# Order of three side works in a long-convolution and low-rank FFN kernel: low-rank steps, modulation rows, kernel reversal

## The chip, the cores and the metric

The kernel runs on one core of a Trainium2 chip. The metric is the device time of one execution in microseconds (us), the median of several runs. Engines are called as in the profile: PE is the matrix engine (TensorE), PEld its weight loads, ACT ScalarE, DVE VectorE, POOL GpSimd, SP the engine that issues most of the DMAs.

## The reference

x has 4 batches of 1024 rows of 2048 columns (4096 rows). Cut to what matters:

```
mod = (silu(c) @ wmod).reshape(4, 6, 1, 2048)      # six sections: sa, ca, ga, sb, cb, gb
ga, gb = sign(.) * max(abs(.), 0.25)
h = layernorm(x) * (1 + ca) + sa
x = x + ga * (causal_conv(h, K) + D * h)           # K: S4 kernel of length 2048, made on the chip
h = layernorm(x) * (1 + cb) + sb
x = x + gb * (h @ W.T + bias + sum_e coeffs_e * scales_e * (h @ A_e.T) @ Bf_e.T)
```

The convolution runs along the 2048 columns of each row. wmod is 2048 by 12288 in 32-bit floats (96 MiB).

## The kernel before

**Blocks.** The 4096 rows are 32 blocks r of 128 rows. A block goes through four works: `stats` (mean and variance, DVE), `conv_prep` (normalize to n, 16 PE transposes tp, ACT scales them to t, ACT and DVE split t and sums of pairs into 16-bit high and low parts hc and hs), `conv_mm` (the convolution as products with Toeplitz tiles) and `conv_post` (store y, square sum on ACT, L660, for the second layernorm). The square of `conv_post` overwrites the block's x, so the next load into that x slot waits for it.

**Convolution.** `conv_mm` works on two halves q. Each half has three families of products: family 0 into ya (L614), copied by ACT to qs (L627); family 2 into yb, summed with qs by DVE (L631); family 1 on top of ya, which must wait for the qs copy. Each product is made of three 16-bit passes. A block has 41,472 columns of 128x128 products. `tick()` is called nine times in a block, and once after it; `PLAN` says what each tick lets in: N (transposes of the next block), S (`step()`), P (`conv_post` of the block before), T and F (statistics and start of block r+2).

**Start.** Blocks 0 to 2 (`EARLY`) are convolved while the modulation rows still stream in. A section of wmod is 16 rows (`mod_load`, 1 MiB each by SP; `mod_mm`, four 32-bit products on PE, L317). Section 1 (ca) comes first. Sections 0 (sa) and 2 (ga) are paced by `pace`: one row per `ROWC` columns of convolution. The row buffers are three in pool wm and two in pool wms; section 2 uses only wm. The convolution kernel is made by `toeplitz`: a load kb from memory (POOL queue), its reversal on PE (kbps, L263) into kb, then the high and low tiles kh and kl (L284, L285). When section 2 is complete, `mod_gate` makes the gate, `gate_tile` spreads it over partitions (gps, L674; gat, L675), `conv_late` (L650, L651) applies it to blocks 0 to 2, and `conv_post` frees their x slots for blocks 4 and on.

**Low-rank work.** `rest()` is a generator of 191 steps: `prep_lora` (la is loaded and squared, L432; lb is loaded by ACT's queue, L441, scaled, L445, and split into lbh and lbl), eight `merge` of 15 steps (products lps with W, split and stored to wcd), and after each second step one row of the modulation sections 4, 3 and 5. `step()` advances it from within the ticks. When it ends, `early()` opens the pools of the FFN. It must have ended by block 30 (`LEFT0`).

**FFN.** From about 960 us on: 16 units of 256 rows by two column halves, seven products each (fX, fY, fZ, L750).

**Order.** A scheduler orders each engine's instructions from the program order, priorities and dependencies. `tc.issue_after(ins)` keeps an instruction behind `ins` if both are on the same engine; it adds no semaphore. Engines take their instructions in order, so one that waits holds what stands behind it.

Of the kernel before, what the change touches and what calls it, by code (L numbers as in the profile page):

```python
# [19 lines left out]
MUL, ADD, SUB = ALU.mult, ALU.add, ALU.subtract  # L20
# [4 lines left out]
P = 128  # L25
# [9 lines left out]
class Net:  # L35
# [288 lines left out]
    def mod_column(self, pool, home, name, plus_one):  # L324

        nc, v = self.nc, self.nc.vector
        row = pool.tile([P, 512], F32, tag="mg0", name="mrow")
        nc.scalar.copy(row, self.modps)
        ps = self.tps.tile([P, 4, P], F32, tag="t", name="mtp")
        for c in range(4):  # L330
            nc.tensor.transpose(ps[:, c, :], row[:, ds(P * c, P)], self.ident)
        col = home.tile([P, NC, NB], F32, tag=name, name=name)
        src = ps.rearrange("p c (q r) -> p q c r", r=32)[:, :, :, 0:NB]
        dst = col.rearrange("p (q c) b -> p q c b", c=4)
        v.tensor_scalar(dst, src, plus_one, None, ADD)
        return col
# [259 lines left out]
    def conv_mm(self, pl, hs, x, tick, early, pace=lambda n: nullcontext()):  # L596
        nc, v = self.nc, self.nc.vector
        hc, hs = hs
        y = pl["y"].tile([P, D], F32, tag="y", name="y")
        yv = y.rearrange("p (j e t) -> p j e t", e=2, t=P)  # L600
        if not early:
            gv = self.gat.rearrange("p (j e t) -> p j e t", e=2, t=P)
        sums = pl["sm"].tile([P, 2], F32, tag="sums", name="sums")

        def family(ps, f, q, first):
            pf = ps.rearrange("p j t -> p (j t)")
            last = 4 * q + 3
            for i in range(last + 1):
                o = P * max(0, i - 4 * q)
                k0 = P * max(0, 4 * q - i)  # L610
                with pace(3 * (512 - o)):
                    for x, z in ((0, 0), (0, 1), (1, 0)):
                        h = hs[x][:, i] if f == 0 else hc[x][:, 2 * i + 2 - f]
                        nc.tensor.matmul(  # L614
                            pf[:, o:512], h, self.kf[f][z][:, ds(k0, 512 - o)],
                            start=first, stop=(i == last and (x, z) == (1, 0)), skip_group_check=True,
                        )
                        first = False
                if i == 3 and q == 1:
                    tick()  # L620

        for q in range(2):
            jj = slice(4 * q, 4 * q + 4)
            pa = self.acc.tile([P, 4, P], F32, tag="a", name="ya")
            family(pa, 0, q, True)
            qs = pl["t"].tile([P, 4, P], F32, tag="qs", name="qs")
            nc.scalar.copy(qs, pa)  # L627
            tick()
            pb = self.acc.tile([P, 4, P], F32, tag="a", name="yb")
            family(pb, 2, q, True)  # L630
            v.tensor_tensor(yv[:, jj, 1, :], pb, qs, ADD)  # L631
            if not early:
                v.tensor_tensor(yv[:, jj, 1, :], yv[:, jj, 1, :], gv[:, jj, 1, :], MUL)
            tick()
            family(pa, 1, q, False)
            sl = ds(1024 * q, 1024)
            if early:
                nc.scalar.copy(yv[:, jj, 0, :], pa)
            else:
                v.tensor_tensor(yv[:, jj, 0, :], pa, gv[:, jj, 0, :], MUL)  # L640
                v.scalar_tensor_tensor(y[:, sl], y[:, sl], 1.0, x[:, sl], MUL, ADD, accum_out=sums[:, q : q + 1])  # L641
            tick()
        return y, sums
# [167 lines left out]
ACC, TPS = 5, 2  # L811
PLAN = ("PNSL", "NL", "NSL", "NTL", "SL", "SL", "SL", "SL", "FSL", "SSL")
LPLAN = ("LL", "LL", "LL", "LL", "L", "0", "")
R0 = 5
WM, WMS = 3, 2
ROWC = 3000
EARLY = 3
X0 = 11
LEFT0 = 30
# [12 lines left out]
def net(ctx: ExitStack, tc: tile.TileContext, io):  # L832
    nc = tc.nc
    k = Net(ctx, tc, io)
# [10 lines left out]
    pl = {}  # L845
# [6 lines left out]
    def section(sec, pools):  # L852
        for q in range(16):
            if q == 0:
                k.mod_begin()
            k.mod_mm(k.mod_load(pools[q % len(pools)], sec, q), q)
            yield
        if sec == 0:
            k.sa = k.mod_column(msm, k.kpool, "sa", 0.0)
            k.hinv = k.fold_scale(msm, k.ca, k.sa, "fs1")  # L860
        elif sec == 1:
            k.ca = k.mod_column(msm, k.kpool, "ca", 1.0)
        elif sec == 2:
            k.gas, (k.gad,) = k.mod_gate(msm, "gad")
        elif sec == 4:
            k.cb = k.mod_column(msm, k.cst, "cb", 1.0)
        elif sec == 3:
            k.sb = k.mod_column(msm, k.cst, "sb", 0.0)
        else:
            _, k.gbd = k.mod_gate(msm, "gbd", io["bias"])  # L870
        yield
# [8 lines left out]
    def take(g, n):  # L880
        for _ in range(n):
            next(g, None)
# [10 lines left out]
    xs, hs, sts, ys = {}, {}, {}, {}  # L893

    def prep(r, shift=True):
        return k.conv_prep(pl, r, xs[r], sts.pop(r), hs, shift)

    def load(r):
        if r < 4:
            with tc.issue_after(k.lastw.ins):  # L900
                xs[r] = k.conv_load(pl, r)
        else:
            xs[r] = k.conv_load(pl, r)

    def stats(r):
        sts[r] = k.stats(pl, xs[r], "1")
# [9 lines left out]
    k.early_scale(msm)  # L916
    load(1)
    rows = (x for sec, w in ((0, (wms, wmp)), (2, (wmp,))) for x in section(sec, w))
    for r in range(2):
        stats(r)  # L920
        take(prep(r, False), 9)
    take(rows, 1)
    with tc.issue_after(k.last.ins), tc.high_priority():
        take(toe, 2)
    take(rows, 1)
    cols = [0]

    def pace(n):

        cols[0] += n  # L930
        while cols[0] >= ROWC:
            cols[0] -= ROWC
            take(rows, 1)
        return tc.issue_after(k.last.ins)

    for r in range(2):
        load(r + 2)
        ys[r] = k.conv_mm(pl, hs.pop(r), xs[r], lambda: None, True, pace)
    stats(2)
    take(prep(2), 9)  # L940
    k.shift_conv(msm)
# [5 lines left out]
    def rest():  # L947
        mods = (x for sec in (4, 3, 5) for x in section(sec, (wmp,)))
        n = 0
        for _ in mer:  # L950
            yield
            n += 1
            if n % MR == 0:
                next(mods, None)
                yield
        for _ in mods:
            yield
        k.ginv = k.fold_scale(msm, k.cb, k.sb, "fs2", k.winv)
        yield

    fill = rest()
    p2l = ExitStack()
    pr, wc, lf = {}, {}, {}
# [15 lines left out]
    def early():  # L979
        right.close()  # L980
        for name, bufs in (("w", 1), ("l", 8), ("t", 1), ("s", 1), ("x2", 1)):
            pr[name] = pool(p2, "p2" + name, bufs, "right")
        load_w(0, ORDER[0])
# [7 lines left out]
    calls = [0]  # L991

    def step():
        calls[0] += 1
        if r < R0 and calls[0] % 2:
            return
        if "w" not in pr and next(fill, 0) == 0:
            early()

    stats(3)  # L1000
# [18 lines left out]
    for r in range(EARLY, 32):  # L1019
# [6 lines left out]
        if r == LEFT0:  # L1026
            while "w" not in pr:
                step()
            lgen = next_left(0)
# [3 lines left out]
        def tick():  # L1033
            for a in next(plan):
                if a == "S":
                    step()
                elif a == "P" and post:
                    k.conv_post(pl, *post)
                elif a == "L" and r >= LEFT0:
                    take(lgen, 1)  # L1040
                elif a == "N":
                    take(nxt, 1)
                elif a == "T" and r + 2 < 32:
                    stats(r + 2)
                elif a == "F" and r + 2 < 32:
                    follow.append(prep(r + 2))
                    take(follow[0], 1)
# [102 lines left out]
```

## Time and profile before

| | |
|---|---|
| median of 3 runs | 2140.63 us (2140.62 to 2143.34) |
| profiled execution | 2145.74 us, its span 2143.8 us |
| PE busy | 2080.1 us, 97% of the span |
| DVE, ACT busy | 1308.9 us (61%), 927.3 us (43%) |
| mean granted PE clock | 0.986 of full speed |
| DMA | 484 MB, 226 GB/s over the span |

The span is from the first to the last instruction. A busy share is an average over stages: the rows, the convolution blocks and the FFN have different limits. In the lists, a number in square brackets is the idle time of the engine ahead of an instruction, with what ended it; a wait line gives who waited for whom, the total, how often, and the longest.

### The profile page before, as it was taken

The numbers are of one execution on the slowest core, as the hardware profiler recorded it, in microseconds if no ns is written. First come the engines' busy times: TensorE is split into PE (matmuls) and PEld (weight loads), VectorE is DVE, ScalarE is ACT, GpSimd is POOL, SyncE is SP. The second block draws the span as 40 slices with busy tenths as digits, with TensorE's granted clock in tenths as the row PEclk, the third lists the DMA queues.
The fourth block names the chain that finished last, engine by engine and source line by source line (L and its number), as shares of the span: only waits on it lengthen the run. The fifth ranks groups of instructions, "written<-read, shape, count | busy, mean of one in ns | idle before, by whom it ended". The sixth has DMA issues, their size and how long they took to land.

```text
span 2143.8 us, 28420 instructions
## 1 busy us (share of the span) xinstructions
PE 2080.1 (97%) x11113; PEld 1026.8 (48%) x11113; DVE 1308.9 (61%) x2351; ACT 927.3 (43%) x1697; POOL 6.2 (0%) x18
## 2 busy tenths in 40 slices
PE   6897999999999999999999999999999999999998
PEld 2343555545455555654545545545444444444444
DVE  5646988998979999666565565565433333332323
ACT  1344776677657877655454454455200000000000
POOL 0000000000000000000000000000000000000000
PEclk8999999999999999999999999999999999999999
DMA  9887667786776454397565564564794545454542
GB/s 383 357 331 266 245 215 277 285 309 255 269 281 238 187 177 168 110 380 265 179 245 189 188 241 181 202 239 177 275 345 164 189 155 166 163 173 162 176 157 69
DMA packets 127236, 484.11 MB, mean 226 GB/s; under 512 B 13608, under 2 KB 13768, under 8 KB 95998
## 3 DMA queue, kind: packets, MB, share of 16 engines
q1 hardware_dynamic: 126192, 477.55, 61.4%
q10 hardware_dynamic: 526, 2.63, 0.3%
q8 instruction: 87, 1.43, 0.3%
q0 software_dynamic: 384, 2.11, 0.2%
q14 instruction: 47, 0.39, 0.1%
HBM read 326.94 MB, written 155.30 MB: 225 GB/s over the span
## 4 chain that ended last, share of the span: by engine, by line
PE 70%; DVE 13%; DMA 8%; ACT 6%; issue 2%; SPq 0%; ACTq 0%; DVEq 0%
PE fZ L750 23%; PE fY L750 15%; PE fX L750 15%; PE ya L614 6%; PE yb L614 3%; PE tp L700 2%; PE modps L317 2%; DMA wm<-in_wmod 2%; PE lps L486 2%; ACT x L660 2%; DVE hc L593 1%; DVE wch L514 1%; ACT t L582 1%; DVE st L540 1%; DVE y L641 1%
## 5 line engine op out<-in xcount | busy, mean ns | idle before, releaser
L750 PEld LDWEIGHTS <-lf 128*128 128x128 f16 x5376 | 526.0, 98 | 620.5 <-issue 0.9
L750 PE MATMUL fZ<-w,lf 128*128 128x512 f16 x2304 | 514.1, 379 | 0.6 <-ACT p L758 0.6
L750 PE MATMUL fX<-w,lf 128*128 128x512 f16 x1536 | 342.1, 379 | 0.0
L750 PE MATMUL fY<-w,lf 128*128 128x512 f16 x1536 | 342.1, 379 | 0.0
L614 PEld LDWEIGHTS <-hc 128*128 128x128 f16 x2304 | 215.9, 98 | 213.6 <-issue 49.1
L768 DVE TENSOR_TENSOR xo<-xo,gb 128x512 f32<-128x512 f32 x128 | 87.5, 689 | 237.6 <-DMA xo<-x1d 225.6
L614 PE MATMUL ya<-kh,hc 128*128 128x512 f16 (+3 forms) x768 | 192.5, 328 | 10.1 <-ACT qs L627 9.9
L582 ACT ACTIVATE t<-tp,sa,ca 128x128 f32<-128x128 f32 x480 | 188.6, 471 | 19.6 <-PE tp L578 19.2
L614 PE MATMUL ya<-kh,hs 128*128 128x512 f16 (+3 forms) x768 | 195.6, 329 | 1.1 <-DVE kh L284 0.6
L614 PE MATMUL yb<-kh,hc 128*128 128x512 f16 (+3 forms) x768 | 194.0, 329 | 1.3 <-DVE y L640 1.2
L758 ACT COPY p<-fZ 128x512 f32<-128x512 f32 x64 | 37.3, 583 | 293.7 <-PE fZ L750 275.3
L614 PEld LDWEIGHTS <-hs 128*128 128x128 f16 x1152 | 107.0, 98 | 111.0 <-issue 35.2
L702 ACT ACTIVATE gt<-tp,sb,cb 128x256 f32<-128x256 f32 x256 | 125.0, 576 | 62.9 <-PE tp L700 61.3
L758 ACT COPY p<-fX 128x512 f32<-128x512 f32 x32 | 18.8, 586 | 305.5 <-PE fX L750 211.2
L317 PE MATMUL modps<-wm,sct 128*32 128x512 f32 x768 | 116.6, 657 | 22.8 <-DMA wm<-in_wmod 22.8
L614 PE MATMUL ya<-kl,hs 128*128 128x512 f16 (+3 forms) x384 | 126.4, 329 | 1.9 <-DVE kl L285 1.9
L614 PE MATMUL yb<-kl,hc 128*128 128x512 f16 (+3 forms) x384 | 126.3, 329 | 0.0
L614 PE MATMUL ya<-kl,hc 128*128 128x512 f16 (+3 forms) x384 | 125.8, 327 | 0.0
L773 DVE TENSOR_TENSOR fin<-fX,gb 128x512 f32<-128x512 f32 x32 | 22.1, 692 | 126.9 <-PE fX L750 126.8
L593 DVE TENSOR_TENSOR hc<-t,hc 128x512 f16<-128x512 f32 x128 | 87.4, 683 | 10.5 <-ACT hc L592 9.9
L578 PE MATMUL tp<-ident,n 128*128 128x128 f32 x512 | 80.6, 284 | 12.1 <-ACT t L582 6.6
L486 PE MATMUL lps<-lbh,lac 128*128 128x512 f16 x256 | 86.3, 379 | 3.1 <-ACT lbh L460 2.4
(265 smaller groups left out, 2220.0 us busy)
## 6 DMA issues: line engine op xcount, KB each, us to landing
wm<-in_wmod SPq DMA_DIRECT2D x96, 1024.0 KB
lfd<-lf SPq DMA_DIRECT2D x112, 512.0 KB
lf<-lfd SPq DMA_DIRECT2D x112, 512.0 KB
x<-in_x SPq DMA_DIRECT2D x32, 1024.0 KB
x1d<-y SPq DMA_DIRECT2D x32, 1024.0 KB
x<-x1d SPq DMA_DIRECT2D x32, 1024.0 KB
xo<-x1d SPq DMA_DIRECT2D x128, 256.0 KB
out<-xo SPq DMA_DIRECT2D x128, 256.0 KB
```

Of the source, the lines that this page charges most:

```text
L317: self.last = self.nc.tensor.matmul(self.modps[32 * g : 32 * g + 32, :], self.sct[:, j].rearrange("p r b -> p (r b)"), w[:, ds(512 * g, 512)],
L486: nc.tensor.matmul(ps, la[:, x, k, h], y[:, k, osl], start=(n == 0), stop=(n == 5))
L578: nc.tensor.transpose(tp[:, k], n[:, ds(P * (c0 + k), P)], self.ident)
L582: nc.scalar.activation(t[:, k], tp[:, k], AF.Identity, bias=self.sa[:, c, b : b + 1], scale=self.ca[:, c, b : b + 1],)
L593: v.tensor_tensor(lo[:, sl], src, hi[:, sl], SUB)
L614: nc.tensor.matmul(pf[:, o:512], h, self.kf[f][z][:, ds(k0, 512 - o)], start=first, stop=(i == last and (x, z) == (1, 0)), skip_group_chec ...
L660: nc.scalar.activation(x, y, AF.Square, bias=mn, accum_out=sq)
L700: nc.tensor.transpose(tp[:, c, r], xs[r][:, ds(P * (c0 + c), P)], self.ident)
L702: nc.scalar.activation(t[:, c0 + c], tp[:, c], AF.Identity, bias=self.sb[:, c0 + c, b : b + 1], scale=self.cb[:, c0 + c, b : b + 1],)
L750: nc.tensor.matmul(ps[name], lf[i][:, k, x, :], wc[i][k // 4][:, k % 4, y, :], start=(first and n == 0), stop=(n == 3 * HC - 1), skip_grou ...
L758: nc.scalar.copy(t, ps[name])
L768: v.tensor_tensor(x, x, self.gbias[:, h], ADD)
```

## The change

1. Low-rank steps. Before, `step()` advanced the low-rank work at every second call while r was under R0 = 5, and at every call from then on. Now, while r is under R0 = 6, it does so at every third call and only for r over `EARLY` = 3, so in blocks 4 and 5; those steps are traced behind the last qs copy (`k.lasta`, ACT) and the last sum (`k.lastv`, DVE) of the running block.
2. Rows. One modulation row per 2400 convolution columns instead of 3000.
3. Reversal. The two toeplitz steps (kbps, and kh and kl) are traced after the transposes of block 0, behind the last transpose of `mod_column`, without high priority; statistics and transposes of block 1 come after them. Before, they came after both blocks and behind the first row of section 0, with high priority.
4. The load of x for blocks 2 and 3 is traced after the convolution of blocks 0 and 1 instead of before it.

```diff
-            nc.tensor.transpose(ps[:, c, :], row[:, ds(P * c, P)], self.ident)
+            self.last = nc.tensor.transpose(ps[:, c, :], row[:, ds(P * c, P)], self.ident)
...
-            nc.scalar.copy(qs, pa)
+            self.lasta = nc.scalar.copy(qs, pa)
...
-            v.tensor_tensor(yv[:, jj, 1, :], pb, qs, ADD)
+            self.lastv = v.tensor_tensor(yv[:, jj, 1, :], pb, qs, ADD)
...
-R0 = 5
+R0 = 6
-ROWC = 3000
+ROWC = 2400
...
-    for r in range(2):
-        stats(r)
-        take(prep(r, False), 9)
-    take(rows, 1)
-    with tc.issue_after(k.last.ins), tc.high_priority():
+    stats(0)
+    take(prep(0, False), 9)
+    with tc.issue_after(k.last.ins):
         take(toe, 2)
-    take(rows, 1)
+    stats(1)
+    take(prep(1, False), 9)
+    take(rows, 2)
...
     for r in range(2):
+        ys[r] = k.conv_mm(pl, hs.pop(r), xs[r], lambda: None, True, pace)
         load(r + 2)
-        ys[r] = k.conv_mm(pl, hs.pop(r), xs[r], lambda: None, True, pace)
...
     def step():
-        calls[0] += 1
-        if r < R0 and calls[0] % 2:
-            return
-        if "w" not in pr and next(fill, 0) == 0:
+        if r < R0:
+            calls[0] += 1
+            if r > EARLY and calls[0] % 3 == 0:
+                with tc.issue_after(k.lasta.ins), tc.issue_after(k.lastv.ins):
+                    next(fill)
+        elif "w" not in pr and next(fill, 0) == 0:
             early()
```

## The prediction

> **What bounds the kernel now.** I read the page first (busy shares), then the stage table (windows), then in the stage with the densest waits the waits of TensorE (PE) and the timelines of ACT, SP and PE. PE is busy 97% of the span:
>
> ```profile
> PE 2080.1 (97%) x11113; PEld 1026.8 (48%) x11113; DVE 1308.9 (61%) x2351; ACT 927.3 (43%) x1697; POOL 6.2 (0%) x18
> ```
>
> The change adds and removes no matrix product, so only PE's idle time (63.7 us) and its slow-clock time can move. The stage table (us, then busy time of PE, PEld, DVE, ACT, POOL, granted clock, DMA share, GB/s) says where they lie:
>
> ```profile
> 0.00:54.00 54.00, 34.14 (x173) 12.28 (x174) 30.69 (x114) 5.91 (x9) 3.58 (x12) 0.80 0.96 382
> 54.00:176.00 122.00, 112.02 (x690) 48.24 (x689) 58.81 (x124) 45.82 (x117) 1.86 (x4) 0.93 0.87 335
> 176.00:214.20 38.20, 26.94 (x145) 12.49 (x142) 28.28 (x64) 18.36 (x26) 0.00 (x0) 0.90 0.74 265
> 214.20:650.00 435.80, 427.03 (x2608) 221.90 (x2608) 385.36 (x809) 308.19 (x631) 0.35 (x1) 0.98 0.72 264
> 650.00:850.00 200.00, 192.74 (x1194) 108.76 (x1187) 189.41 (x408) 147.04 (x305) 0.41 (x1) 1.00 0.54 200
> 850.00:960.00 110.00, 109.56 (x647) 61.57 (x646) 72.22 (x130) 69.71 (x136) 0.00 (x0) 1.00 0.60 230
> ```
>
> Until 54 nothing is edited. In 54 to 176 the 32 weight rows of sections 0 and 2 stream in beside blocks 0 to 2: PE idles 10.0 us. In 176 to 214 (block 3) it idles 11.3 of 38.2 us, the worst stretch. From 214 to 960 it idles 16.5 us in 746; the FFN after 960 is untouched. Block 3, PE's waits (total, times, longest), then ACT, SP and PE in time:
>
> ```profile
> PE ya L614 <- ACT qs L627: 6.8, 1, 6.8
> PE tp L578 <- DVE n L557: 3.3, 1, 3.3
> ...
> 177.60 0.43 ACTq L441 DMA_DIRECT2D lb<-in_BfT  x1
> 178.08 0.59 ACT L638 COPY y<-ya 128x512 f32<-128x512 f32 x1 [0.28 <-PE gps L674]
> 189.34 2.00 ACT L445 ACTIVATE lb<-lb,lwt 128x2048 f32<-128x2048 f32 x1 [10.68 <-DMA lb<-in_BfT]
> 191.25 0.57 ACT L627 COPY qs<-ya 128x512 f32<-128x512 f32 x1
> ...
> 195.69 1.99 ACT L660 ACTIVATE x<-y,mn 128x2048 f32<-128x2048 f32 x1
> ...
> 197.80 0.35 SPq L562 DMA_DIRECT2D x<-in_x  x1
> ...
> 191.86 0.59 PE L614 MATMUL ya<-kh,hc 128*128 128x512 f16 x1 [6.75 <-ACT qs L627]
> ```
>
> The low-rank preparation (prep_lora) put L445, which needs the 2 MiB load of lb, ahead of block 3's qs copy. ACT stood 10.7 us; qs, ready to be copied when PE stopped at 185.1, ran at 191.25, and PE stood 6.75 us. It also held back L660 (its input mn was there at 188.8; it ran at 195.69), after which alone the next input tile x can load (197.80). That load feeds block 4's statistics, n, and the transposes at 214.2, where PE waits again.
>
> **What the Trainium skill says.** "TensorE: Matmul & The Clock Gate", Part 1 (the HAM clock gate): after an idle window of about 3.4 us PE runs at half rate until it has been busy as long. The trace agrees: after the 6.75 us gap a 128x512 matmul takes 0.63 us instead of 0.38, until 196.6; gaps of 0.6 to 1.5 us at 105 to 123 (PE 75% busy) left the clock at 1.00. "DMA: Bandwidth & Descriptors", Where 436 GB/s comes from: 435 GB/s is the ceiling of a core's ports. The trace's full slices show 415 to 431, so a 1 MiB row costs at least 2.47 us.
>
> **The change, part by part.**
>
> (1) *Low-rank steps.* A block calls step() 9 times. Before, blocks 3, 4, 5 advanced the low-rank work by 4, 5, 9 steps; now by 0, 3, 3: 12 of its 191 steps come later, and it ends in block 26 instead of 25. In the order of the changed program la's squares (L432) stand at block 4's end, lb's load right behind them, and L445 only behind block 5's second qs, some 20 us later, so the 10.7 us transfer is covered by block 5. The DVE instructions L437 (stood 5.2 us for lws at 163 to 168) and L52 to L438 also leave block 3; all its other ACT and DVE instructions keep their order.
>
> Time of block 3 from its gate product (gps, G=176.05) to the transposes of block 4 (214.2), before: 38.15 us. After, on DVE from the timeline's durations: two gat 2.7 (first gps done at G+1.2), L650 4.0, two gat 5.5, L651 6.7, two L650 9.1, two L651 11.5, mn 11.6 (before 12.7). ACT is free: L660 and its accumulator read, 2.18, end at 13.8 (before 21.8): 8.0 us earlier. The load then takes as long as before, at most 7.0 us (197.80 to the statistics at 204.82): 20.6. From the first bn_stats to the end of n DVE takes 9.3 us (204.82 to 214.14): 29.9. **Gain 38.15 - 29.9 = 8.2 us.** PE's own work there is gps and first part 12.9, rest of the convolution 8.4, three rows 3.2: 24.5. So what is late next is n, and PE will wait about 5.4 us at block 4's transposes. Bounds: 13.6 us if only PE's work counted, 4 us if the load lands 4 us later in a busier DMA queue.
>
> Added waits: the steps' ACT and DVE instructions in blocks 4 and 5 queue behind lasta and lastv. Behind them wait only later low-rank work, and on ACT block 5's qs behind L432 (3.8 us); PE has yb's 1.6 us before it needs that: 0 to 2.2 us, taken 0, as ACT is 68% busy there. The first lps product waited 2.45 us for lbh; now its last half of lbl stands behind block 6's last sums, about 4.5 us against 3.2 us of rows and transposes on PE: 1.3 to 3, taken 2: **-0.5 us.** Every DMA of the steps (la and lb 2 MiB each, we, wm rows) moves along with them; SP's queue in blocks 4 and 5 holds only x loads and y stores and four rows. In block 26 the 12 steps fall into 850 to 960, where DVE is 66% and PE idles 0.4 us of 110: nothing. The number of full blocks (some 20) and so their about 1 us of idle each (7.3 in 200 us) stays. That cover gone, it costs 1 to 2 us.
>
> (2) *A row per 2400 columns.* A block has 41,472 convolution columns; 32 rows took 96,000, now 76,800. PE per row: 2400 columns at 0.427 ns (32,256 took 13.77 us after the last row), 1.02, and the row itself 1.06: 2.1 us, under the 2.47 us that DMA needs. So DMA bounds this stage and PE waits about 0.5 us per row. Before, from row 0 (58.16) to row 31 (161.2) DMA moved 34 MiB in 103 us, 11.8 of them idle; 2.68 each otherwise. Now 33 MiB (the x of block 3 falls behind the rows), with about half of the idle time (the hole at 69 to 75 shrinks as row 2 no longer stands behind the first convolution pieces; the one at 135 to 141 shrinks as gsp is split): 33 x 2.68 + 6 = 94.4, so the last row ends at 153.7. Behind it are 51,456 columns (22.0 us) and 16 transposes (2.1): gps at 177.8, **+1.7 us.** Bounds: -3 (no DMA holes) to +6 (holes as before).
>
> (3) *Reversal behind the first transposes.* kbps now runs when kb lands (47.34 + 10.1 = 57.4) rather than behind row 0. But ACT's second kb copy is queued behind the last group of block 0's transposes, so kh comes at about 69.0 (before 68.1) and kl ends at 71.5 (before 71.06). PE does row 2 meanwhile. 0, between -2 and +2.
>
> (4) *Later x loads.* x of block 2 goes behind 16 more rows on SP; its n is ready about 0.8 us after PE asks: hidden by the DMA wait of the next row. x of block 3 is issued behind the last row; it needs 2.7 us to land, then 5.5 for statistics and n and about 5 of the gate's and L414's DVE work, against 10.9 us of columns ahead of its transposes: 0 to +2.5, taken 0. On POOL kb and gsb keep their places.
>
> Sum: -8.2 - 0.5 + 1.7 = -7.0. The profiled execution took 2145.74 (span 2143.8 and 1.9 around it) and becomes 2138.7; the median shown is 5.1 lower, so 2140.63 - 7.0 = **2133.6 us.**
>
> **The rivals.**
> - *The rows cost what block 3 wins* (chance 0.20). For it: DMA share 0.87 already in 54 to 176. Against: the holes come from PE's late release of row buffers, which denser rows relieve. With +6 instead of +1.7 and n late by 2: 2140.
> - *The clock falls in the row stage, slower* (0.13). PE will be about 75% busy between 90 and 150. At 42 to 54 it was 60 to 63% busy and the clock 0.65 to 0.72; at 75% it held. A cold episode costs about 2.5 us (192 to 198 at 0.62) of 6; three eat the gain, and six give 2133.6 + 15 = 2149. It decides from three on.
> - *The stall stays in another place* (0.05): lb's load runs into block 5 or 6 and L445 again holds a qs. For it only that the transfer took 10.7 us; against, some 20 us of ACT work in between. 2141, no change.
>
> **How the numbers follow.** 0.2% (4.3 us) is about what a measurement of this kernel tells from no change. The likeliest case (0.62) has its own range 2126 to 2136. The row rival is half a step inside no change (0.15 of its 0.20, the rest faster); the lb rival 0.03 no change, 0.02 slower; the clock rival slower. Faster 0.67, same 0.18, slower 0.15. The range 2124 to 2145 leaves out the clock rival and a tail below.
>
> **What would show it.** ACT's wait for lb of 10.7 us and PE's 6.8 us for qs vanish; x for block 4 is issued about 14 us after gps, not 21.8; PE then waits some 5 us for n; gps starts at 175 to 181; PE's waits for wm after 54 grow from 5.8 us to 9 or more. Wrong if PE's clock between 90 and 150 falls under 0.9, if gps starts after 182, or if 214 to 960 (746 us, 16.5 of idle) changes by over 4 us.

## The result and the profile after

The changed kernel takes 2140.32 us (median of 20 runs), the kernel before 2142.42 us in its 20 runs beside them. The ratio is 0.9994 with a 95% interval of 0.9985 to 1.0003: no change that the measurement can tell (one disturbed run of 2204 us is left out of the ratio; the others lie between 2134.8 and 2146.6). Forecast was 7.0 us less. The profiled execution took 2140.44 us, its span 2138.5 us. It lies at its kernel's median; the profiled execution of the kernel before (2145.74) lies 3.3 us above the median of 20 runs, so not all of the 5.3 us between the two spans is the change's.

The busy shares, then the rows of the stage table (length, busy time of PE, PEld, DVE, ACT, POOL, granted clock, DMA share, GB/s):

```profile
PE 2078.8 (97%) x11113; PEld 1024.8 (48%) x11113; DVE 1309.8 (61%) x2351; ACT 925.3 (43%) x1697; POOL 6.2 (0%) x18
```

```profile
54.00:176.00 122.00, 105.77 (x651) 43.21 (x650) 55.99 (x117) 39.47 (x107) 1.86 (x4) 0.94 0.90 349
176.00:214.20 38.20, 32.09 (x187) 16.75 (x184) 32.63 (x71) 12.74 (x25) 0.00 (x0) 0.96 0.57 209
214.20:650.00 435.80, 428.60 (x2617) 223.76 (x2617) 385.38 (x814) 315.37 (x644) 0.34 (x1) 0.99 0.70 262
650.00:850.00 200.00, 194.50 (x1203) 108.51 (x1202) 193.10 (x410) 154.92 (x319) 0.41 (x1) 1.00 0.57 213
850.00:960.00 110.00, 109.56 (x641) 60.98 (x639) 73.06 (x129) 66.90 (x125) 0.00 (x0) 1.00 0.62 239
```

The windows stand still while the work moved, so what the rows tell is the idle time: in 54 to 176 PE idles 16.2 us where it idled 10.0, and in 176 to 214.2 only 6.1 where it was 11.3. What block 3 won, the row stage lost. From 214.2 to 960 PE idles 13.1 us in place of 16.5. From the first mtp (PE's transposes behind section 1) to gps PE runs 693 matmuls in both profiles and is busy 113.1 us before and 112.7 after; the 6 us between them are idle time (10.0 and 16.2 us).

The last row, gps and block 4's transposes on PE before:

```profile
161.22 1.06 PE L317 MATMUL modps<-wm,sct 128*32 128x512 f32 x8 [0.26 <-DMA wm<-in_wmod]
...
176.05 1.94 PE L674 MATMUL gps<-mg,ident 128*128 128x512 f32 x4
...
214.20 1.97 PE L578 MATMUL tp<-ident,n 128*128 128x128 f32 x8 [3.28 <-DVE n L557]
```

After, PE's waits from 54 to block 4's first transposes, then PE, ACT, SP and DVE in time (start, duration, instruction, in brackets the idle time ahead of it and what ended it):

```profile
PE modps L317 <- DMA wm<-in_wmod: 7.8, 6, 3.0
PE tp L578 <- DVE n L557: 6.1, 1, 6.1
PE kbps L263 <- DMA kb<-kd: 4.1, 1, 4.1
PE ya L614 <- DVE kh L284: 2.6, 1, 2.6
```

```profile
58.87 6.34 PE L263 MATMUL kbps<-kb,rev 128*128 128x512 f32 x8 [4.06 <-DMA kb<-kd]
...
157.19 1.06 PE L317 MATMUL modps<-wm,sct 128*32 128x512 f32 x8 [0.91 <-DMA wm<-in_wmod]
...
182.16 1.94 PE L674 MATMUL gps<-mg,ident 128*128 128x512 f32 x4
...
193.70 2.00 ACT L660 ACTIVATE x<-y,mn 128x2048 f32<-128x2048 f32 x1 [5.53 <-DVE mn L658]
...
195.82 0.35 SPq L562 DMA_DIRECT2D x<-in_x  x1
...
210.90 1.33 DVE L557 TENSOR_SCALAR n<-x,mv,rs 128x2048 f32<-128x2048 f32 x1
...
212.28 1.97 PE L578 MATMUL tp<-ident,n 128*128 128x128 f32 x8 [6.11 <-DVE n L557]
```

The two stalls of block 3 are gone: no wait of ACT for lb, no 6.8 us of PE for qs. L660 now waits only for mn, x is loaded 13.7 us after gps, and block 4's transposes start 30.1 us after gps (38.15 before, 29.9 forecast). But gps starts at 182.16, not at 176.05 (before) or 177.8 (forecast). So block 4 starts only 1.9 us earlier. The forecast had it at 177.8 + 29.9 = 207.7, which is 6.5 us earlier. The last row ends at 158.25 where 153.7 was forecast; the stretch behind it is the forecast's (23.9 us against 24.1). The question is the row stage.

### The profile page after: what moved, and what is told of

Same layout as the page of the kernel before. It is cut to its first block, busy times and chain, and to the rows that moved or that the text cites. A ratio compares the mean times of both kernels' runs of the same rounds, so it can differ in the third digit from the quotient of the medians.

```text
span 2138.5 us, 28420 instructions
## 1 busy us (share of the span) xinstructions
PE 2078.8 (97%) x11113; PEld 1024.8 (48%) x11113; DVE 1309.8 (61%) x2351; ACT 925.3 (43%) x1697; POOL 6.2 (0%) x18
## 4 chain that ended last, share of the span: by engine, by line
PE 57%; issue 25%; DVE 3%; DMA 2%; ACT 1%; POOLq 0%; SPq 0%; POOL 0%; DVEq 0%
PE fZ L750 23%; PE fY L750 15%; PE fX L750 15%; PE tp L700 2%; PE ya L614 1%; DMA gb<-gbd 1%; PE yb L614 1%; DMA w<-wcd 0%; DVE y L641 0%; ACT x L660 0%; DMA x<-x1d 0%; DVE wch L514 0%; DVE lf L713 0%; DVE st L540 0%; DVE y L640 0%
## 5 line engine op out<-in xcount | busy, mean ns | idle before, releaser
L317 PE MATMUL modps<-wm,sct 128*32 128x512 f32 x768 | 118.4, 666 | 24.2 <-DMA wm<-in_wmod 24.1
```

Source lines behind the costliest of these rows:

```text
L317: self.last = self.nc.tensor.matmul(self.modps[32 * g : 32 * g + 32, :], self.sct[:, j].rearrange("p r b -> p (r b)"), w[:, ds(512 * g, 512)],
```

## The experiments

Theory A: the low-rank steps win what was forecast, and one of the other edits gives it back in blocks 0 to 2. Its rivals change in the course of the runs. Each kernel was timed beside the kernel before. Single executions reach the first mtp at 50.8 to 54.6 us, and one profile is one draw; so the table counts from that mtp, and the ratios, not the profiles, decide. The last three columns are us: from the first mtp to the end of the last row, from there to gps, and from gps to block 4's first transposes.

| kernel | steps | columns per row | reversal | x loads | ratio to before (95%) | mtp to last row's end | to gps | to block 4's tp |
|---|---|---|---|---|---|---|---|---|
| before | old | 3000 | old | old | 1 | 109.3 | 13.8 | 38.1 |
| changed | new | 2400 | new | late | 0.9994 (0.9985 to 1.0003) | 105.0 | 23.9 | 30.1 |
| e8, the same | new | 2400 | new | late | 0.9994 (0.9986 to 1.0003) | 103.6 | 25.5 | 30.2 |
| e1 | new | 3000 | old | old | 0.9967 (0.9956 to 0.9979) | 107.8 | 13.6 | 31.0 |
| e2 | old | 2400 | new | late | 0.9992 (0.9980 to 1.0004) | 105.3 | 29.3 | 30.6 |
| e3 | new | 3000 | new | late | 0.9982 (0.9974 to 0.9991) | 112.0 | 14.8 | 31.1 |
| e4 | new | 2400 | old | late | 0.9986 (0.9977 to 0.9996) | 99.7 | 24.8 | 30.0 |
| e5 | new | 2400 | old | old | 0.9993 (0.9984 to 1.0001) | 107.3 | 21.7 | 30.8 |
| e6 | new | 3000 | new | old | 0.9969 (0.9957 to 0.9981) | 109.6 | 13.6 | 29.9 |
| e7 | new | 3000 | old | late | 0.9965 (0.9953 to 0.9977) | 109.9 | 14.8 | 30.6 |
| e9 | new | 3400 | old | old | 0.9939 (0.9927 to 0.9952) | 110.1 | 8.4 | 29.3 |
| e10, five buffers | new | 2400 | new | late | 0.9975 (0.9967 to 0.9982) | 101.1 | 24.9 | 30.4 |
| e11, half rows | new | 2400 | new | late | 0.9943 (0.9925 to 0.9960) | 91.0 | 25.8 | 31.9 |
| e12 | new | 3700 | old | old | 0.9960 (0.9947 to 0.9973) | 114.3 | 4.2 | 30.7 |
| e13 | new | 3400 | new | late | 0.9988 (0.9978 to 0.9997) | 124.2 | 8.4 | 29.0 |
| e14 | old | 3400 | old | old | 0.9994 (0.9986 to 1.0002) | 108.4 | 8.4 | 36.7 |
| e15 | new | 3400 | new | old | 0.9958 (0.9944 to 0.9971) | 109.4 | 8.4 | 30.2 |
| e16 | new | 3400 | old | late | 0.9992 (0.9985 to 0.9998) | 118.0 | 8.4 | 29.8 |

0.001 of the ratio is 2.1 us. Every kernel with the new steps has 29 to 32 us from gps to block 4.

### e1 to e4: the steps alone, and the change with one part taken back

e1 is the kernel before with the steps only; e2 is the changed kernel with the old `step()` and R0; e3 and e4:

```diff
-ROWC = 2400
+ROWC = 3000
```

```diff
-    stats(0)
-    take(prep(0, False), 9)
-    with tc.issue_after(k.last.ins):
-        take(toe, 2)
-    stats(1)
-    take(prep(1, False), 9)
-    take(rows, 2)
+    for r in range(2):
+        stats(r)
+        take(prep(r, False), 9)
+    take(rows, 1)
+    with tc.issue_after(k.last.ins), tc.high_priority():
+        take(toe, 2)
+    take(rows, 1)
```

> The kernel before with the low-rank steps alone changed (no step in block 3, three each in blocks 4 and 5); rows at 3000 columns, reversal and x loads as before. Theory A (the steps win what was forecast, the new row stage of blocks 0 to 2 gives it back): block 3's gate product starts where it did (176 +-1.5 us), from it to block 4's first transposes about 30 us in place of 38.2, and the time is 7 to 8.5 us below before (ratio 0.9960 to 0.9967): faster than the whole change. Rival B (the steps win nothing in the end, since the low-rank work or another wait comes late elsewhere): ratio 0.999 to 1.000, with the same 30 us in block 3 and 5 to 8 us more in 214 to 960.

> The whole change without its low-rank part: rows at 2400 columns, new place of the reversal, later x loads, but the old steps. Theory A: gate product at 181 to 183 us, the 38 us to block 4's transposes back, and the time 5 to 6 us above before (ratio 1.0023 to 1.0028). Rival B: gate product late as well, but the time within 2 us of before, since the stage's delay is absorbed later. Rival C (the gate product's 182 in the one profile was scatter, the row stage costs nothing): 177 to 179 and ratio 1.000 to 1.001.

> The whole change with 3000 columns per row again. If the denser rows are what makes blocks 0 to 2 late (the forecast's rival), the gate product comes back to about 176 to 177 us and the ratio to before is 0.9965 to 0.9975. If the reversal's new place (kb waited for at about 59 us, first rows of section 0 seven us later) is what costs, 3000 columns make it later still, 182 to 185 us, and the ratio is 0.999 to 1.001.

> The whole change with the old order around the reversal: both blocks' transposes first, a row ahead of the reversal. If the reversal's new place costs the 4 to 5 us by which the last row came later than worked out, row 0 runs at 58 to 63 us again, the last row ends at about 154, the gate product starts at 177 to 178.5 us and the ratio to before is 0.9962 to 0.9972. If the denser rows cost it, the gate product stays at 181 to 183 us and the ratio at about 0.999.

e1, PE in time:

```profile
161.07 1.07 PE L317 MATMUL modps<-wm,sct 128*32 128x512 f32 x8 [0.75 <-DMA wm<-in_wmod]
...
175.72 1.94 PE L674 MATMUL gps<-mg,ident 128*128 128x512 f32 x4
...
206.70 1.97 PE L578 MATMUL tp<-ident,n 128*128 128x128 f32 x8 [6.97 <-DVE n L557]
```

The steps alone win 0.0033, 7.1 us: theory A holds for them, rival B falls. e3 and e4 lie between: taking back one edit of the changed kernel gains 2.6 us (the row pace, e3) or 1.7 us (the reversal, e4), with intervals too wide to blame one of them. The profile of e4 looked like a full recovery (gps at 176.8), but it was the fastest of its 17 runs (2136.8 us; median 2141.0): a warning against reading a cause from one profile. e2 lands on rival B's number, for a reason that neither theory had. In its trace the old low-rank steps stand in another place: the squares of la (L432) stood on ACT at 172.6, in front of block 3's t, PE waited 2.3 us for t and then ran at half clock from 177 to 180; gps came at 188.1 in this profile (2148.39 us, 4.8 over e2's median), but the lb stall behind it was gone. The gain of the steps and the cost of the rest are tied to each other.

### e5 to e8: one edit each on top of the steps

e5 adds `ROWC = 2400` to e1, e6 the new place of the reversal, e7 the late x loads; e8 is the changed kernel again.

> The kernel before with the new low-rank steps and 2400 columns per row; reversal and x loads as before. The steps alone gave 0.9967 (-7.1 us). Theory C (the reversal's new place is what gives the gain back; denser rows cost 1 to 2 us): last row ends at 152 to 154 us, gate product at 176 to 178, ratio 0.9967 to 0.9978. Rival D (the denser rows give it back by themselves): last row at 157 to 159, gate product at 181 to 183, ratio 0.999 to 1.000.

> The kernel before with the new low-rank steps and the reversal behind the first block's transposes; rows at 3000 columns, x loads as before. Theory C: TensorE waits 2 to 4 us for kb at about 59 us, row 0 runs at about 65.5 us in place of 58 to 63, the last row ends 4 to 5 us later than with the steps alone (166 in place of 162), the gate product at 180 to 181 and the ratio is 0.9985 to 0.9995. Rival D: row 0 as late, but the delay is taken up before the gate product, and the ratio stays at 0.9965 to 0.9975.

> The kernel before with the new low-rank steps and the x loads of blocks 2 and 3 behind the convolutions of blocks 0 and 1. If the later loads cost what was taken at nothing (0 to 2.5 us): block 2's or block 3's transposes wait for n at most 1 us more, the gate product at 175 to 178 us, ratio 0.9967 to 0.9978. If they are what gives the gain back, the transposes wait 4 us or more for n, the gate product comes at 180 or later and the ratio is 0.9985 or above.

> The changed kernel once more, beside the three others on the same chip, for a second profile and a second median. If its first profile was typical: row 0 at about 65.5 us, last row at 158, gate product at 181 to 183, 30 us from there to block 4's transposes, ratio 0.9985 to 1.0003. If the first profile was a late one, the gate product comes at 177 to 179 and the ratio falls to 0.998 or below.

The row pace alone brings e1's 0.9967 to 0.9993: 5.6 us. Neither the reversal (0.9969) nor the x loads (0.9965), each added alone, cost anything at 3000; with both (e3, 0.9982) it is 2.8 to 3.6 us more than with one, by intervals that overlap. Theory C falls, rival D holds for e5 and e6. In e6 PE waited 0.9 us for kb and row 0 ran late (64.6), and the time did not move. PE's waits in e5:

```profile
PE modps L317 <- DMA wm<-in_wmod: 9.9, 10, 4.0
PE tp L578 <- DVE n L557: 9.6, 3, 6.8
```

The rows are waited for 9.9 us in e5 and 4.7 us in e1. In the changed kernel much the same time is split differently: 7.8 for rows, 4.1 for kb. From the first mtp to gps the profiles of the changed kernel, e8 and e5 need 129.0 to 129.2 us, with either place of the reversal (e4's, its fastest run, 124.5). e8's second draw has row 0 at 62.6, the end of the last row at 154.8 and gps at 180.3, 1.8 to 3.5 us earlier than the first, and earlier than expected; its first mtp came 2.0 us earlier. It gives the ratio of the first, so the first profile was typical. PE idles 16.2, 16.1 and 17.4 us on the way in the changed kernel, e8 and e5 (13.3 in e4): where PE waits differs, how long hardly does. That points at the transfers.

### e10 and e11: what bounds the dense rows

e10 gives section 2 five row buffers; e11 loads half of each row of sections 0 and 2 and reads that half twice:

```diff
-    rows = (x for sec, w in ((0, (wms, wmp)), (2, (wmp,))) for x in section(sec, w))
+    rows = (x for sec, w in ((0, (wms, wmp)), (2, (wms, wmp))) for x in section(sec, w))
```

```diff
-        self.lastw = self.nc.sync.dma_start(out=w, in_=src[:, j, ds(sec * D, D)])
+        d = D // 2 if sec in (0, 2) else D
+        self.half = d < D
+        self.lastw = self.nc.sync.dma_start(out=w[:, 0:d], in_=src[:, j, ds(sec * D, d)])
...
-                w[:, ds(512 * g, 512)],
+                w[:, ds(512 * (g % 2 if self.half else g), 512)],
```

> The whole change, with five row buffers instead of three in section 2 (the pool of section 0 used as well); every engine's instructions stand in the same order as in the changed kernel. Theory F with transfer holes (the 129 to 138 us hole, some 4 to 5 us of DMA idle, comes because three buffers stand full while TensorE does the shift's products): the hole shrinks to 2 us or less, the last row ends 2 to 4 us earlier after the first mtp (101 to 103 us in place of 103.6 to 105), gate product as much earlier, ratio 0.9975 to 0.9985. Rival H (transfers at their ceiling, holes don't matter): nothing moves, ratio 0.999 to 1.000.

> The whole change with half of each row's bytes loaded in sections 0 and 2 (1024 of 2048 columns; the products read that half twice, so TensorE's work and order are the same; the modulation it computes is another one). If the transfers bound the row stage at 2400 columns per row, TensorE's waits for rows vanish (7 to 10 us to under 2), the last row ends some 8 to 12 us earlier and first mtp to gate product falls from 129 to 119 to 122 us; ratio 0.995 to 0.997. If TensorE's own order, the reversal or the columns behind the last row set the time, it stays at 126 to 129 us and 0.998 to 1.000.

With half the bytes the ratio is 0.9943, 10.9 us under the changed kernel. The stage table of e11 in 54 to 176, to be set against the changed kernel's row above:

```profile
54.00:176.00 122.00, 116.23 (x719) 48.43 (x720) 61.67 (x124) 42.72 (x115) 1.61 (x4) 0.99 0.65 227
```

DMA is busy 0.65 instead of 0.90, PE idles 5.8 us instead of 16.2, and the first mtp to gps takes 116.7 us instead of 129, more than was expected. It is not a pure test: against what was expected the scheduler put PE's instructions in another order (the gsp products, small ones that work out how the shift sa passes the convolution, stand behind the last row), and the clock stayed higher (0.99 instead of 0.94). But nearly all of the waits for rows went (1.4 us left), and PE's idle time fell by 10.5 us. With more buffers and the same order on every engine, 4 us come back (0.9975, its interval apart from the changed kernel's): the last row ends 101.1 us after the first mtp (105.0 and 103.6 with three). The hole that three buffers leave, in 3 us windows of the changed kernel (the last but one column is the DMA share):

```profile
129.00:132.00 3.00, 3.00 (x28) 2.52 (x24) 0.00 (x0) 1.56 (x3) 0.00 (x0) 1.00 0.61 178
132.00:135.00 3.00, 2.73 (x13) 0.54 (x13) 1.72 (x5) 0.41 (x1) 0.53 (x1) 0.58 0.48 194
135.00:138.00 3.00, 3.00 (x17) 0.72 (x15) 0.00 (x0) 0.00 (x0) 0.56 (x1) 0.85 0.83 279
```

PE is all but full there (with the gsp products, and from 132 to 135 at a clock of 0.58), frees rows late, and the queue stands 3.2 us of these nine (some 2 us of such a hole are left in e10, from 133 to 139). Summed over 1 us windows from about 5 us after the first mtp to the last row, DMA stood idle 15.0 us before, 11.4 in the changed kernel, 13.6 in e5 and 9.5 in e10, with 86 to 89 us of transfers in each. So transfers and their holes set the end of the rows at 2400 columns, and behind them lie 51,456 columns with less left to load (the DMA share of 176 to 214 fell from 0.74 to 0.57).

### e9 and e12: slower rows

e9 and e12 are e1 with `ROWC = 3400` and `ROWC = 3700`.

> The kernel before with the new low-rank steps and 3400 columns per row in place of 3000. Theory F (the row stage is set by how evenly TensorE's columns lie under the transfers: at 2400 the rows come faster than the queue delivers and 51,456 columns are left behind the last row with nothing to load): fewer waits for rows than with the steps alone at 3000 (4.7 us), last row at 164 to 168 us, gate product at 173 to 176, ratio 0.9955 to 0.9970. Rival G (the pace itself doesn't matter, only what PE waits for at the start): gate product at 176 to 178 and a ratio as at 3000 and 2400 alike, 0.997 to 1.000. From some pace on the rows must come too late for the gate: if 3400 is beyond it, last row to gate product falls to 5 us or less and the ratio rises to 0.998 or above.

> The kernel before with the new low-rank steps and 3700 columns per row. Theory F: 30 paced rows take 111,000 of the 124,416 columns of blocks 0 to 2, so about 5 us of columns are left behind the last row, still enough for the gate's chain of about 3 us: waits for rows fall further, gate product at 172 to 176 us, ratio 0.995 to 0.997. If the pace is too slow there, the gate product waits for the last row or for the gate chain and comes at 178 us or later, ratio 0.998 or above.

e9, PE in time:

```profile
161.58 1.07 PE L317 MATMUL modps<-wm,sct 128*32 128x512 f32 x8 [1.59 <-DMA wm<-in_wmod]
...
171.02 1.94 PE L674 MATMUL gps<-mg,ident 128*128 128x512 f32 x4
...
200.30 1.97 PE L578 MATMUL tp<-ident,n 128*128 128x128 f32 x8 [5.26 <-DVE n L557]
```

e9 takes 2128.39 us (median of 5), 13 us under the kernel before: faster than both kernels, the best version found. Its last row ends as long after the first mtp as before (110.1 against 109.3 us), but only 8.4 us of work are left behind it instead of 13.8. The ratio is under the range expected, and the waits for rows did not fall as theory F had it (4.7 us, as in e1). A shorter rest behind the last row goes with the gain; that it is the cause is not shown. In e9 gps comes 118.4 us after the first mtp, in e1 121.4. PE does the same work on the way, idles 7.8 us (8.3 in e1) and is busy 110.6 us (113.2), at a mean clock of 0.95 (0.93): most of these 3 us are clock. Another 1.7 us are a shorter wait for n.

At 3700 the rest shrinks to 4.2 us, but the last row comes 4 us later, and the ratio is 0.9960: e12 seems to gain less than e9 (the intervals just overlap), though gps came as early (171.7). Its remaining blocks from block 4 on took 1933.0 us, e9's 1929.8. Its trace has a longer wait for block 4's n (8.3 us against 5.3), half clock behind it until 212 us (e9 until 207), and a further slow stretch at 270 to 274 us; what sets these off is not traced.

### e13 to e16: the best pace in the other kernels

e13 is the changed kernel with 3400, e14 the kernel before with 3400; e15 and e16 are e13 with the old x loads and with the old place of the reversal.

> The whole change with 3400 columns per row in place of 2400: new steps, reversal behind the first transposes, later x loads. The new steps with 3400 and the old reversal and x loads gave 0.9939. Theory F (the pace alone gave the gain back; what TensorE waits for kb at the start counts only where transfers don't bind): 2 to 4 us worse than that at most, gate product at 172 to 176 us, ratio 0.994 to 0.996. Rival I (reversal and x loads together cost as much as the pace, as the 0.9982 of the whole change at 3000 may mean): gate product at 178 us or later, ratio 0.9975 or above.

> The kernel before with 3400 columns per row and nothing else. If the gain of the steps (-7.1 us at 3000) and that of the slower pace (another -5.9 at 3400) add, this one is 5 to 7 us below before: ratio 0.9967 to 0.9977, gate product at 171 to 174, 38 us from there to block 4's transposes. If they are tied to each other, as the low-rank steps stood before and not behind the gate product in the kernel with dense rows and old steps, the ratio is 0.998 to 1.001.

> New steps, 3400 columns per row, reversal behind the first transposes, but the x loads ahead of the convolutions as before. In the whole change at 3400 (0.9988) block 3's n stood on VectorE behind the sums with gsb (L414), which waited 11.6 us for the broadcast of gsb, and TensorE waited 12.0 us for n. Theory J (the late x load of block 3 is what puts n behind L414): with the early load n is at about 130 us, ahead of L414, the 12 us wait is gone, gate product at 171 to 174 us, ratio 0.994 to 0.996. Rival K (the reversal's new place costs it): gate product at 178 us or later, ratio 0.998 or above.

> New steps, 3400 columns per row, later x loads, but the reversal in its old place. Theory J: block 3's n stands behind L414 again, TensorE waits 5 to 12 us for it at 149 to 161 us, gate product at 178 us or later, ratio 0.9975 to 0.9995. Rival K: n behind L414 as well, but without the 5 us wait for kb at the start the gate product comes at 172 to 175 us and the ratio is 0.994 to 0.996.

Theory F, that only the pace counts, fell with e13. DVE of e13 in time, then PE:

```profile
153.38 4.50 DVE L414 TENSOR_TENSOR y<-y,gsb 128x2048 f32<-128x2048 f32 x2 [11.55 <-DMA gsb<-gsd]
...
159.16 1.35 DVE L557 TENSOR_SCALAR n<-x,mv,rs 128x2048 f32<-128x2048 f32 x1
```

```profile
160.65 1.09 PE L578 MATMUL tp<-ident,n 128*128 128x128 f32 x4 [11.96 <-DVE n L557]
```

The late x load puts block 3's n behind the sums with gsb on DVE, and those stand for the broadcast of gsb, which POOL issued at 144.7 into a full DMA queue (a share of 0.95 to 1.05 from 144 to 153) and which landed 8.6 us later. With the early load n is there long before (e15):

```profile
132.13 1.34 DVE L557 TENSOR_SCALAR n<-x,mv,rs 128x2048 f32<-128x2048 f32 x1
```

e15 comes to 0.9958, e16 stays at 0.9992 (there PE waited 6.7 us for that n): theory J holds. At 2400 the same wait (11.66 us in the changed kernel) stands before L414 as well, but ends at 145.6, when block 3's transposes are 23 us off. The late x loads are free at 2400 (e4 against e5) and, with the old reversal, at 3000 (e7 against e1), and cost 6 to 11 us at 3400 (e13 against e15, e16 against e9). The reversal costs e15 against e9 some 4 us, with intervals that overlap.

e14, with the old steps, shows the stall for lb in a new place. gps came at 168.3, the earliest of all, and then the lb load held not ACT but SP, in whose queue the next x load stood. SP's waits, and SP and PE in time:

```profile
SPq L352 <- DMA lb<-in_BfT: 10.0, 1, 10.0
```

```profile
189.37 0.37 SPq L562 DMA_DIRECT2D x<-in_x  x1
```

```profile
204.96 1.97 PE L578 MATMUL tp<-ident,n 128*128 128x128 f32 x8 [12.43 <-DVE n L557]
```

x left 21.1 us after gps, as in the kernel before (21.8). By the ratio the gain of the pace is gone (0.9994), but the profile does not lose it here: block 4 still starts 9.2 us earlier than before (204.96 against 214.20). It is lost between block 4's first transposes and block 10's. Before, then e14:

```profile
214.20:358.00 143.80, 139.28 (x840) 73.95 (x841) 129.04 (x277) 101.38 (x213) 0.35 (x1) 0.97 0.67 247
204.96:361.09 156.13, 145.45 (x841) 76.59 (x841) 129.75 (x282) 108.14 (x223) 1.15 (x1) 0.93 0.60 224
```

For the same work PE idles 10.7 us instead of 4.5 there and is busy 6.2 us longer at a lower mean clock, part of it behind the 12.43 us wait. (This profile is the slowest of e14's 13 runs, 4.3 us over their median, so a typical run loses less.) What delays blocks 4 to 9 was not traced. By the ratios pace and steps do not add: of the kernels tried, the slower pace pays only where the low-rank steps are out of block 3.

## Why the forecast was wrong

- **Step (1), the low-rank steps: right.** gps to block 4's transposes 30.1 us (29.9 forecast), x issued 13.7 us after gps (13.8), PE's wait for n 6.1 us (5.4). Alone they are worth 7.1 us; the forecast had a gain of 8.2 less 0.5. From block 4 to 960 us nothing was lost, as worked out. (The sum has a slip: 13.8 + 7.0 is 20.8 and not 20.6, so it comes to 30.1, the measured figure.)
- **Step (2), a row per 2400 columns: the step that failed.** It was sized at +1.7 us and cost 5.6 us on top of the steps alone (e5 against e1; taken back in the changed kernel, where the other edits stay, it gains 2.6, e3). The kind was right: transfers bound the stage (e11), about 24 us of columns lie behind the last row. The term that failed is the idle time of DMA, taken as half of before because denser rows were to relieve the late release of row buffers. Counted as in the forecast, 11.8 us became 10.5 and not 6 (the sum starts at 153.7 - 94.4 = 59.3; from there to 158.25, less 33 times 2.68). That puts the last row 4.5 us late, and gps with it. In the finer count above 15.0 us became 11.4, and 13.6 in e5. With two more buffers for section 2, 4 us came back (e10). The upper bound given, "+6 (holes as before)", has the size that was measured (gps 6.1 us later), though the holes did shrink a little. A small slip changes nothing: at the fastest slice shown (431 GB/s) a row takes 2.43 us, not 2.47.
- **Step (3), the reversal: right at 0 for the change's effect, wrong in its picture.** kbps did wait 4.1 us for kb, and row 0 ran 7 us later than before; at 2400 it cost nothing that the ratios tell (e4: 1.7 us, overlapping), and with the old x loads nothing at 3000 (e6). With the late x loads at 3000 (e3 against e7) and at 3400 (e15 against e9) it may cost 4 us; the intervals overlap. At 2400 PE waits for rows otherwise (9.9 us in e5), which is the likely reason.
- **Step (4), later x loads: right at 0** at this pace, and on the edge: at 3400 PE waits for the n that stands behind L414 (e13, e16).
- **The rivals.** What happened is the first one, "the rows cost what block 3 wins" (2140 us, chance 0.20). Its price (+6 in place of +1.7) was right, and its addition that n comes 2 us late was not needed. The clock did not fall between 90 and 130 us (1.00); it did at 132 to 135 and at 147 to 150 (0.58), as before at 135 to 141 (0.51). PE was 89% busy between 90 and 150, not 75%; the 75% given for 105 to 123 before is 83% in the profile. The lb stall did not come back in the changed kernel, only in e14. The forecast named a gps after 182 us as the sign of being wrong: it came at 182.16. PE's waits for rows rose to 7.8 us, and to 11.9 with the wait for kb; at least 9 had been named.

"TensorE: Matmul & The Clock Gate", Part 1, of the Trainium skill fits here too: behind the 6.97 us wait for n in e1 the clock is 0.50 from 205 to 215 us and full again from 216; PE is busy without a break from 211. Summed over 1 us windows that is 3.6 us of PE's work lost behind a 7 us wait: about half as much again. An idle window does not explain every fall: at 138 to 141 before, behind the gsp products, the clock is 0.50 although PE is busy all the time and idled only 0.4 us since 123. No run here tells why.

What stays open: why the slower pace gains in e9, the 4 us between e9 and e15, what lengthens the waits in e12 behind the last row and in e14 in blocks 4 to 9, and why the old steps land elsewhere in e2 and e14 (only their traces were read).

## What to carry to other kernels

When side transfers stream under compute, look at both ends: denser rows brought more waits for rows (9.9 us in e5, 4.7 in e1) and left 22 us of work behind the last row in place of 14. Find the best pace by trial: here it was 3400, while 3700 gained no more, though its gate came as early, and in the changed kernel 3400 won nothing over 2400 that the intervals tell (e13). Size such a stage by its transfers plus the holes that full buffers leave, and take the holes as they are until a buffer is added. Edits that share a queue need not add: test each on top of the others, trust medians over one profile, and follow a gain past the place where it was made (e14 kept it until block 4 and had lost it by block 10).

## What was not expected of the hardware

One and the same kernel reaches the same place up to 2 us apart: the first mtp of the changed kernel started at 53.2 us in one profile and at 51.2 us in the other, and its times spread over 12 us (2134.8 to 2146.6), while those of e9 spread over 5.5 us (2126.6 to 2132.1, five runs). Half the bytes of 32 rows (16 of 32 MiB, e11) were worth 11 us in a stage whose DMA share was 0.90, not 1: here a queue that was not full all the time was the bound, with holes while the row buffers waited for PE (two more buffers gave 4 us back, e10).
